# The stretch between the experts and the attention: pair swap by a DVE shuffle instead of copies, and a new order of key pieces, sums, tables and heads

## The chip, the cores and the metric

The kernel runs on one core of a Trainium2 chip, in one launch. The metric is the device time of one execution in microseconds (us). One execution was taken with the profiler; all durations and positions below are of that execution, counted from the start of its span.

The engines are named as the profile names them: PE (TensorE, matrix products; PEld is its weight load), DVE (VectorE), ACT (ScalarE), POOL (GpSimd) and SP (the queue from which most transfers are issued). Each engine works through its own list of instructions in the order in which the program wrote them, and waits on semaphores where an operand or a buffer is not ready.

## The reference

Two decoder layers with a layer norm behind each of six blocks, on `x` of 4 x 512 x 256 and a context of 4 x 1601 x 256, all in float32:

```python
x = _layernorm(x + _L0_attn_ref(...))    # per-token gradient steps
x = _layernorm(x + _L0_xattn_ref(...))   # one-head attention over the context
x = _layernorm(x + _L0_ffn_ref(...))     # 8 experts, 2 per token, each with its own norm
x = _layernorm(x + _L1_attn_ref(...))    # causal self attention, 16 heads of 16
x = _layernorm(x + _L1_xattn_ref(...))   # 16 heads, rotated queries and keys
x = _layernorm(x + _L1_ffn_ref(...))     # dequantized weights
```

The case is about the border between the third block and the next two. An expert's output is normalized and scaled with its own gamma and beta, and each token sums the rows of its two experts. In the fifth block, queries and keys of every head are rotated, where neighbouring rows are swapped in pairs (the sign is folded into the table of sines):

```python
def apply_rope(x, cos, sin):
    x2 = jnp.stack([-x[..., 1::2], x[..., 0::2]], axis=-1).reshape(x.shape)
    return x * cos + x2 * sin
```

## The kernel before, in words

Everything is written for a manual schedule: the order in which the Python code emits an instruction is its order on its engine. Line numbers are those of the kernel before.

**Experts.** Rows are sorted by expert and worked off in 23 blocks of 256 rows (`E + NDYN`). The loop runs `first_half` (both input products, gelu and sigmoid) of one block, `turned` of the next and `second_half` of the one before. `second_half` evicts the output product (L899), normalizes (L903), applies gamma and beta on POOL (L909, L910) and stores the block to `ys` from SP's queue (L911). After each `second_half` one step of the generator `attention_first` is run (`next(more, None)`): it prepares what attention needs. A step reaches to the next `yield`; there are 22 calls in the loop, and what is left of the generator runs behind the last block. Among its last steps are `live` (L989), `xa_bo` (L996) and `bob` (L1000), each a small product on PE and an eviction on DVE. Earlier steps load the context of batch 0 into the buffers `qt` and `ks`, load the rotation tables of batch 0 into `turn` buffers (the idle `xT` tiles), and fill `ng`, `vs` and `v` with memsets on POOL.

**Behind the experts.** The code at L1593 onwards writes out by hand:

- `fetch`: eight gathers on POOL of the rows of `ys` for batch 0 (tiles `ex`); `first_sums`: gathers and sums for batch 1, on POOL alone.
- the loads of the tables `c_cos` and `c_sin` (1601 columns each) on SP's queue.
- the values of batch 0 (13 tiles; L1196 copies each out on ACT).
- `keys0`, eight key pieces of batch 0: chunks 0 to 3 of the context with two pieces `c` each. `keys0[0:2]` and `[4:6]` read chunks 0 and 2, which lie in the buffers of heads' groups 0 and 1; `[2:4]` and `[6:8]` read chunks 1 and 3, in those of groups 2 and 3.
- `values1`, 13 value tiles of batch 1, from chunks `cx` (two buffers) that SP loads two ahead.
- `add`: the two weighted expert rows summed into `x` of batch 0 on DVE (L1091), with statistics (L156), root (`sd`, `rstd` on ACT, L125 and L127) and scaling on ACT; `turn`: its transposes.
- `k0_`, `q0_`, `k1_`, `q1_`: projections of self-attention keys and queries, halves 0 and 1 of the heads; each is stored to DRAM from a `raw` tile, and `rows0`, `rows1` read it back in the layout by heads, on SP's queue. `self_values(0)`: four value tiles.

**A key piece** (`key` in `context`) is a product on PE, an eviction with bias on ACT into a `raw` tile (four buffers), the rotation (`rotated`), and later a store of `raw` to `kcd` in DRAM from SP. `flush(1)` at the head of each piece issues the stores of all but the newest finished piece; `flush(0)` issues all. `rotated` fills `swp` (two buffers) with the rows of `raw` swapped in pairs, and then does two products with the tables and a sum. These three run on DVE for batch 0 and on POOL for all others and for the queries (24 key pieces and 8 queries).

**Attention.** 32 units (`units`): four head groups of four batches, first self attention, then cross attention. For each unit `slot1` computes scores only for their maxima, on PE and DVE (L1274 self, L1272 cross; tiles `one`, four banks), a few slots ahead of the unit's own scores, exponentials (L1329, ACT) and weighted sums (L1342). Other work is put into lists by unit, `extras[i]`, and run between the slots; among it are the key pieces of batches 1 to 3 (`keys1`, `later`) and the cross queries. The maxima, exponentials and these pieces share the engines in the order written.

Of the kernel before, what the change touches and what calls it, by code (L numbers as in the profile page):

```python
# [17 lines left out]
P = 128  # L18
# [21 lines left out]
def decoder(ctx: ExitStack, tc: tile.TileContext, a: dict, out: bass.AP):  # L40
# [748 lines left out]
    def const(pool, name, shape, queue):  # L789
        t = pool.tile(shape, F32, tag=name, name=name)  # L790
        queue.dma_start(t, a[name])
        return t
# [28 lines left out]
    with tc.tile_pool(name="p3", bufs=2) as p3, ExitStack() as ordered:  # L821
# [70 lines left out]
        def second_half(i, wo, xb, g):  # L892
            ps = bank()
            pv = ps.rearrange("p (h d) -> p h d", d=D)
            for h in range(2):
                blk = slice(h * P, (h + 1) * P)
                mm(pv[:, h, :], [(g[:, f, blk], wo[:, f * D : (f + 1) * D]) for f in range(NF)])
            r = p3.tile([P, 2, D], F32, tag="rb", name="rb")
            nc.vector.tensor_tensor(r, pv, xb, ALU.add)  # L899
            mv = moments(r, 2)  # L900
            rs = rstd_of(mv, eps12, 2)
            for h in range(2):
                nc.vector.tensor_scalar(  # L903
                    r[:, h, :], r[:, h, :], mv[:, h, 0:1], rs[:, h : h + 1], ALU.subtract, ALU.mult
                )
            gam, bet = (
                wo[:, None, (NF + k) * D : (NF + k + 1) * D].to_broadcast([P, 2, D]) for k in (1, 2)
            )
            nc.gpsimd.tensor_tensor(r, r, gam, ALU.mult)  # L909
            nc.gpsimd.tensor_tensor(r, r, bet, ALU.add)  # L910
            nc.sync.dma_start(ys[i * BLK : (i + 1) * BLK, :].rearrange("(h p) d -> p h d", p=P), r)  # L911

        def attention_first():
# [5 lines left out]
            ready["later"] = p4a.tile([P, 2 * P], BF16, tag="later", name="later")  # L919
            yield  # L920
            nc.gpsimd.tensor_copy(ready["later"], later)
            yield
            qt, ks = ready["qt"], ready["ks"] = [group_tiles(p4a, n, S) for n in ("qt", "ks")]

            at = qt + ks
# [24 lines left out]
            for i in range(2 * NT):  # L950
                t = p4a.tile([P, 4, 32], F32, tag=f"ng{i}", name=f"ng{i}")
                nc.gpsimd.memset(t, 0.0)
                ngs.append(t)
            yield
            ready["vself"] = [values_tile(p4a, f"vs{i}", NT) for i in range(2)]
            yield
            ready["vals"] = [values_tile(p4a, "v0", NKT)]
            yield

# [68 lines left out]
    with ExitStack() as s4:  # L1028
# [118 lines left out]
        def rotated(raw, n, ks, eng, tables=None):  # L1147

            cos, sin = tables or (cosT[:, ks], sinT[:, ks])
            swp = p4.tile([P, S + 1], F32, tag="swp", name="swp")[:, :S]  # L1150
            pairs = raw.rearrange("(a two) n -> a two n", two=2)
            into = swp.rearrange("(a two) n -> a two n", two=2)
            for i in range(2):
                nc.sync.dma_start(into[:, i, :n], pairs[:, 1 - i, :n])
            eng.tensor_tensor(raw[:, :n], raw[:, :n], cos[:, :n], ALU.mult)  # L1155
            eng.tensor_tensor(swp[:, :n], swp[:, :n], sin[:, :n], ALU.mult)
            eng.tensor_tensor(raw[:, :n], raw[:, :n], swp[:, :n], ALU.add)
# [442 lines left out]
            f()  # L1600
        for f in first_sums:
            f()
        cosT = const(p4c, "c_cos", [P, S2], nc.sync)
        sinT = const(p4c, "c_sin", [P, S2], nc.sync)
        for f in context(0, (), range(4), here=qt + kself):
            f()

        keys0 = context(0, range(4), (), here=qt + kself)
        (k0_, q0_), rows0 = self_rows(0, 0)
        (k1_, q1_), rows1 = self_rows(0, 1)  # L1610
        for f in keys0[0:2] + keys0[4:6] + values1[:6] + add + values1[6:] + turn:
            f()
        for f in (k0_, q0_, rows0, *keys0[2:4], *keys0[6:8], *self_values(0), k1_, q1_, rows1):
            f()
        flush(0)
        for i, (n0, n1) in enumerate(((0, 4), (4, 6), (6, 7), (7, 8))):
            extras[i] = keys1[n0:n1] + extras[i]
        later = [
            context(2, range(4), ()) + context(3, range(2), ()),
            context(3, range(2, 4), ()) + context(2, (), range(4)),  # L1620
# [238 lines left out]
```

## Time and profile before

| what | us |
|---|---|
| median of three runs | 2454.46 (2454.04 to 2455.28) |
| profiled execution: its own time | 2460.01 |
| profiled execution: its span | 2458.2 |
| PE busy | 2349.0 |
| DVE busy | 1187.0 |
| ACT busy | 1074.2 |
| POOL busy | 425.0 |
| mean granted TensorE clock | 0.964 of full speed |
| experts' last product on PE begins | 1013.1 |
| first self-attention maximum on DVE | 1101.6 |

The span runs from the first to the last instruction. A busy PE includes matmuls that wait in its pipeline, and at a lower granted clock the same matmul is busy for longer; so idle PE time and the clock are read together. A row of the timeline gives start, duration, engine, line, operation, output and inputs, and in brackets how long the engine had been idle before it and what ended that. Rows with SPq are issues of transfers: a long one or a late one means that the queue was waiting. Idle time of an engine that no other waits for costs nothing.

### The profile page before, as it was taken

What the parts mean: (1) busy time and instruction counts of PE and PEld (TensorE: products, weight loads), DVE (VectorE), ACT (ScalarE), POOL (GpSimd) and SP (SyncE); (2) the same over time, 40 slices, a digit from 0 to 9 for tenths busy, and PEclk for the clock granted to TensorE, in tenths of its full rate; (3) what the DMA queues carried; (4) which work ended last, traced back from release to release, by engine and by line L of the source; (5) the groups of instructions that cost most, each with busy time, mean ns of one, the idle gap of its engine ahead of it and who ended that gap; (6) DMA issues with size and microseconds to landing.
All of it is one profiled execution on the core that took longest, in us unless ns stands there. A gap on an engine that the chain in (4) does not pass through costs nothing.

```text
span 2458.2 us, 34942 instructions
## 1 busy us (share of the span) xinstructions
PE 2349.0 (96%) x13928; PEld 1331.3 (54%) x13928; DVE 1187.0 (48%) x2772; ACT 1074.2 (44%) x1996; POOL 425.0 (17%) x431
## 2 busy tenths in 40 slices
PE   7998999959999999969999999999999999999998
PEld 4767677748888888743333334333333333333256
DVE  1333334422222222336666667666666666677334
ACT  1111222114455544324555553655566565556730
POOL 1010001121134444323330000222110010000000
PEclk9999999969999999978999998999999999999999
DMA  8300211234767555442211220122210110110100
GB/s 319 135 1 23 102 54 44 73 135 149 263 251 273 212 190 197 145 122 81 83 44 30 71 75 5 49 73 62 66 54 20 44 40 16 32 36 16 33 9 26
DMA packets 82513, 224.50 MB, mean 91 GB/s; under 512 B 14120, under 2 KB 37934, under 8 KB 73262
## 3 DMA queue, kind: packets, MB, share of 16 engines
q1 hardware_dynamic: 68190, 141.70, 17.1%
q0 software_dynamic: 10992, 65.54, 7.3%
q10 hardware_dynamic: 3168, 15.03, 1.8%
q8 instruction: 110, 1.80, 0.3%
q14 instruction: 53, 0.43, 0.1%
HBM read 171.53 MB, written 53.21 MB: 91 GB/s over the span
## 4 chain that ended last, share of the span: by engine, by line
PE 51%; ACT 1%; DVE 1%; issue 0%; DVEq 0%; ACTq 0%
PE s L1315 23%; PE one L202 12%; PE po L1342 11%; PE s L202 2%; PE s L1325 1%; PE one L1300 1%; PE one L1363 1%; ACT x L171 0%; ACT ex L1329 0%; DVE one L1274 0%; PE one L1384 0%; PE one L1405 0%; PE one L1482 0%; DVE pm L1272 0%; DVE st L156 0%
## 5 line engine op out<-in xcount | busy, mean ns | idle before, releaser
L1329 ACT ACTIVATE ex<-s 128x512 f32<-128x512 f32 (+1 forms) x1062 | 578.1, 594 | 480.5 <-PE s L1315 237.4
L1272 DVE TENSOR_REDUCE pm<-one 128x1 f32<-128x512 f32 x768 | 494.2, 686 | 203.7 <-PE s L1315 147.7
L1315 PE MATMUL s<-q,kc 32*128 32x512 f32 x1612 | 522.9, 640 | 0.2 <-ACT ex L1329 0.2
L202 PE MATMUL one<-kc,qt 32*128 32x512 f32 (+1 forms) x2048 | 483.6, 563 | 0.3 <-DVE pm L1272 0.3
L1315 PEld LDWEIGHTS s<-q,kc 32*128 32x128 f32 x1612 | 161.6, 179 | 210.2 <-issue 175.2
L1342 PE MATMUL po<-ex,v 128*32 128x256 f32 (+3 forms) x2472 | 245.8, 466 | 0.3 <-ACT ot L1355 0.3
L1274 DVE CUSTOM_DVE_ANT_0 one<-one,c_diagq 128x512 f32<-128x512 f32 x256 | 172.0, 716 | 89.2 <-PE one L202 78.3
L1315 PE MATMUL s<-q,ks 32*128 32x512 f32 x512 | 182.2, 660 | 4.9 <-ACT ex L1329 4.9
L1342 PEld LDWEIGHTS po<-ex,v 128*32 128x32 f32 (+1 forms) x2472 | 49.9, 108 | 233.0 <-issue 227.0
L886 DVE TENSOR_TENSOR g<-g,sg 128x1024 f32<-128x1024 f32 x46 | 57.3, 1246 | 238.3 <-ACT sg L883 238.3
L202 PE MATMUL wide<-xbT,eWi 128*128 128x256 f32 x736 | 168.4, 388 | 4.0 <-DVE xbT L858 4.0
L202 PEld LDWEIGHTS one<-kc,qt 32*128 32x128 f32 x2048 | 163.9, 188 | 11.7 <-DVE pm L1272 7.7
L202 PE MATMUL bank<-eWo,g 128*128 128x256 f32 x736 | 162.8, 379 | 0.5 <-DVE rb L899 0.5
L202 PE MATMUL wide<-xbT,eWg 128*128 128x256 f32 x736 | 162.9, 379 | 0.1
L202 PEld LDWEIGHTS wide<-xbT,eWi 128*128 128x128 f32 x736 | 143.6, 195 | 25.1 <-issue 3.4
L1155 POOL TENSOR_TENSOR raw<-raw,c_cos 128x512 f32<-128x512 f32 (+1 forms) x32 | 35.0, 1093 | 696.2 <-DMA swp<-raw 616.5
L202 PE MATMUL one<-ks,qt 32*128 32x512 f32 x512 | 153.4, 668 | 1.1 <-ACT raw L1126 1.1
L202 PEld LDWEIGHTS wide<-xbT,eWg 128*128 128x128 f32 x736 | 139.8, 190 | 19.5 <-ACT g L883 0.5
L202 PEld LDWEIGHTS bank<-eWo,g 128*128 128x128 f32 x736 | 138.1, 190 | 18.5 <-DVE rb L899 0.6
L883 ACT ACTIVATE g<-wide,eWi 128x256 f32<-128x256 f32 x184 | 71.9, 477 | 69.8 <-PE wide L202 67.0
L1315 PEld LDWEIGHTS s<-q,ks 32*128 32x128 f32 x512 | 54.1, 188 | 83.1 <-issue 61.9
L202 PE MATMUL wide<-ctxT,q 128*128 128x512 f32 (+1 forms) x256 | 91.3, 510 | 0.8 <-DVE q L649 0.8
(310 smaller groups left out, 2969.7 us busy)
## 6 DMA issues: line engine op xcount, KB each, us to landing
xs<-zero SPq DMA_DIRECT2D x32, 512.0 KB
kc<-kcd SPq DMA_DIRECT2D x16, 800.5 KB
eWo<-in_eWo SPq DMA_DIRECT2D x8, 1408.0 KB
cx<-in_ctxT SPq DMA_DIRECT2D x18, 512.0 KB
eWi<-in_eWi SPq DMA_DIRECT2D x8, 1028.0 KB
eWg<-in_eWg SPq DMA_DIRECT2D x8, 1028.0 KB
swp<-raw SPq DMA_DIRECT2D x64, 128.0 KB
qt<-qd SPq DMA_DIRECT2D x32, 256.0 KB
```

The lines of the kernel that those rows point to most:

```text
L202: nc.tensor.matmul(ps, l, r, start=(i == 0), stop=(i == n - 1))
L883: nc.scalar.activation(dst[:, k, :], pv[:, k, :], func, bias=bias)
L886: nc.vector.tensor_tensor(part, part, dst, ALU.mult)
L1155: eng.tensor_tensor(raw[:, :n], raw[:, :n], cos[:, :n], ALU.mult)
L1272: nc.vector.tensor_reduce(pm[:, t, j, c : c + 1], ps, AX.X, ALU.max)
L1274: nc.vector.tensor_tensor_reduce(out=ps, in0=ps, in1=diagq[:, 384 - t * P : 896 - t * P], scale=1.0, scalar=LOWEST, op0=ALU.add, op1=ALU.m ...
L1300: nc.tensor.transpose(pt[:, t * P : (t + 1) * P], ng.rearrange("p j r -> p (j r)"), ident)
L1315: nc.tensor.matmul(ps[:kn], kt[rows, k * P : k * P + kn], q2[rows, :], start=True, stop=cross)
L1325: nc.tensor.matmul(ps[:, k * P : (k + 1) * P], later_[:, :P], later_[:, P:], start=False, stop=True)
L1329: nc.scalar.activation(ex[:kn, h, :], ps[:kn], AF.Exp)
L1342: nc.tensor.matmul(state["po"][j * 32 : j * 32 + 32, q0:q1], (vals if cross else vself)[b % 2][:kn, k, c0 : c0 + 32], ex[:kn, j % 2, q0:q1 ...
L1363: nc.tensor.transpose(pt[:, t * P : (t + 1) * P], ot[:, t * P : (t + 1) * P], ident)
```

## The change

Five edits, all at this border but for the last, which also reaches into attention:

- three `yield`s of `attention_first` are taken out, so that its last steps come three blocks earlier, and the memsets of `ng`, `vs` and `v` run in one step;
- the last block's gamma and beta are applied on DVE;
- the sums of batch 0 (`add`) follow two key pieces and all of `values1`; the other two pieces of groups 0 and 1 come behind the sums; self values come ahead of the remaining four key pieces, and `k1_`, `q1_`, `rows1` move into the first unit's `extras`;
- the tables `c_cos` and `c_sin` are loaded behind the last key piece of batch 0;
- `rotated` swaps the pairs with one `stream_shuffle` on DVE from `raw` to `swp` instead of two transfers on SP's queue, in all 40 rotations.

```diff
-            nc.gpsimd.tensor_tensor(r, r, gam, ALU.mult)
-            nc.gpsimd.tensor_tensor(r, r, bet, ALU.add)
+            eng = nc.vector if i == E + NDYN - 1 else nc.gpsimd
+            eng.tensor_tensor(r, r, gam, ALU.mult)
+            eng.tensor_tensor(r, r, bet, ALU.add)
...
             nc.gpsimd.tensor_copy(ready["later"], later)
-            yield
             qt, ks = ready["qt"], ready["ks"] = [group_tiles(p4a, n, S) for n in ("qt", "ks")]
...
                 ngs.append(t)
-            yield
             ready["vself"] = [values_tile(p4a, f"vs{i}", NT) for i in range(2)]
-            yield
             ready["vals"] = [values_tile(p4a, "v0", NKT)]
             yield
...
             swp = p4.tile([P, S + 1], F32, tag="swp", name="swp")[:, :S]
-            pairs = raw.rearrange("(a two) n -> a two n", two=2)
-            into = swp.rearrange("(a two) n -> a two n", two=2)
-            for i in range(2):
-                nc.sync.dma_start(into[:, i, :n], pairs[:, 1 - i, :n])
+            nc.vector.stream_shuffle(swp[:, :n], raw[:, :n], [i ^ 1 for i in range(32)])
             eng.tensor_tensor(raw[:, :n], raw[:, :n], cos[:, :n], ALU.mult)
...
-        cosT = const(p4c, "c_cos", [P, S2], nc.sync)
-        sinT = const(p4c, "c_sin", [P, S2], nc.sync)
         for f in context(0, (), range(4), here=qt + kself):
             f()
...
-        for f in keys0[0:2] + keys0[4:6] + values1[:6] + add + values1[6:] + turn:
+        for f in keys0[0:2] + values1 + add + keys0[4:6] + turn:
             f()
-        for f in (k0_, q0_, rows0, *keys0[2:4], *keys0[6:8], *self_values(0), k1_, q1_, rows1):
+        for f in (k0_, q0_, rows0, *self_values(0), *keys0[2:4], *keys0[6:8]):
             f()
+        cosT = const(p4c, "c_cos", [P, S2], nc.sync)
+        sinT = const(p4c, "c_sin", [P, S2], nc.sync)
         flush(0)
         for i, (n0, n1) in enumerate(((0, 4), (4, 6), (6, 7), (7, 8))):
-            extras[i] = keys1[n0:n1] + extras[i]
+            extras[i] = ([k1_, q1_, rows1] if i == 0 else []) + keys1[n0:n1] + extras[i]
```

## The prediction

> **What bounds the kernel now.** The page first (busy rows and slices), then the table of windows, then the timeline of the one place where the slices show a hole. In the page:
>
> ```profile
> PE 2349.0 (96%) x13928; PEld 1331.3 (54%) x13928; DVE 1187.0 (48%) x2772; ACT 1074.2 (44%) x1996; POOL 425.0 (17%) x431
> ...
> PE   7998999959999999969999999999999999999998
> ...
> PEclk9999999969999999978999998999999999999999
> ```
>
> TensorE is the bound nearly everywhere. The edit's place is the hole at slices 17 and 18, between experts and attention. The windows there (columns: window, length, busy PE, PEld, DVE, ACT, POOL, clock, DMA share, GB/s):
>
> ```profile
> 1020.00:1030.00 10.00, 6.88 (x19) 4.28 (x18) 3.30 (x10) 2.33 (x4) 3.95 (x5) 0.69 0.08 26
> ...
> 1050.00:1060.00 10.00, 3.62 (x17) 2.91 (x16) 6.75 (x10) 0.98 (x3) 6.11 (x7) 0.90 0.65 192
> 1060.00:1070.00 10.00, 3.84 (x9) 2.56 (x9) 6.29 (x16) 3.32 (x10) 8.45 (x10) 0.50 0.09 27
> ...
> 1080.00:1090.00 10.00, 6.24 (x24) 3.47 (x22) 0.00 (x0) 1.93 (x3) 0.00 (x0) 0.93 0.62 193
> ```
>
> From 1010 to 1130 TensorE is idle for 23.0 us (the sum of 10 minus PE busy over the twelve windows), and its clock is down to 0.50. What ends the idle times, from the timeline (start, duration, instruction, [idle before <- releaser]):
>
> ```profile
> 1025.48 5.03 PE L202 MATMUL one<-xaV,qt 128*128 128x256 f32 x11 [0.61 <-DVE bob L1000]
> ...
> 1059.66 3.75 PE L202 MATMUL one<-xaV,cx 128*128 128x256 f32 x8 [6.38 <-DMA cx<-in_ctxT]
> ...
> 1066.39 0.30 ACT L125 ACTIVATE sd<-mv,eps 128x4 f32<-128x4 f32 x1 [14.44 <-DVE mv L161]
> ...
> 1069.57 5.49 PE L202 MATMUL one<-xaV,cx 128*128 128x256 f32 x12 [6.16 <-ACT v L1196]
> ...
> 1087.06 1.91 SPq L1154 DMA_DIRECT2D swp<-raw  x2
> ...
> 1091.33 0.32 ACT L1187 ACTIVATE raw<-one,bk 128x65 f32<-128x65 f32 x1 [5.58 <-DMA kcd<-raw]
> 1091.70 4.02 PE L202 MATMUL one<-qkvV,xT 128*128 128x256 f32 x8 [4.76 <-ACT raw L1187]
> ...
> 1101.64 0.69 DVE L1274 CUSTOM_DVE_ANT_0 one<-one,c_diagq 128x512 f32<-128x512 f32 x1
> ```
>
> Four stalls: (1) the experts' leftovers (`live`, `xa_bo`, `bob`) hold the first value matmul until 1025.5; (2) 6.4 us for a context chunk, whose load stood on SP's queue behind `swp` copies that waited; (3) 6.2 us for ScalarE, stopped 14.4 us at `sd` because the expert sums stand in the middle of `values1`; (4) 4.8 us because `raw`'s four buffers come free only after `kcd<-raw`, which stood behind `rows0` and `swp` copies. 1101.64, the first self-attention maximum, is my finish mark.
>
> **The change, part by part.** I walk the new order with the old durations.
>
> *Three fewer yields.* `live`, `xa_bo` and `bob` ran behind the last expert and now fall into its loop. Their matmuls cost about 1.4 us there at full clock (two of 0.39 to 1.14 us and one of 1.02 at the gap's low clock), so the last expert's product, 7.17 us from 1013.1, ends near 1020.7 instead of 1020.2; its eviction (0.69 us) frees the bank and values start near 1021.4 instead of 1025.5. Thirteen value tiles took 13.9 us at a clock partly of 0.69; at 0.86 each, as `cx` tiles took at 1046, they take 11.2: done 1032.6 (was 1039.3). The merged POOL step puts 1.23 us of `ng` memsets and about 1.1 of `vs` and `v` ahead of one weight fetch instead of three; POOL sat over 9 us waiting for each `eWo`, and TensorE had no such wait. Cost 0; if that cover were gone, 1 us once. The `ctxT` loads on ScalarE's queue go one expert earlier: 0.
>
> *Last gamma and beta on DVE.* 2 x 0.69 (the `raw<-raw,xT` row) for 2 x 1.27 on POOL. With the later product `ys` is issued near 1025.5, not 1026.1: gathers 0.6 us earlier.
>
> *Sums behind two key pieces; shuffle.* Two key pieces (4 matmuls of 0.43 each, 1.75): 1036.1. DVE rotates each with a shuffle and three 0.69 operations: done 1040.7. `values1`'s first chunk to 1039.6; the third chunk's load is issued at once, since no copy stands before it on SP, and lands 3 to 4 us later: stall about 1 us instead of 6.4; `values1` done 1048.4. The sums (6.5 us on DVE, 1059.5 to 1066.0) run beside it from 1040.7 to 1047.2; the last gather is in by 1040. Root and four scalings (1066.4 to 1069.3 on ACT, 2.9 us, behind the last `v`) end at 1051.7, as TensorE ends the other two key pieces (1051.9): stall (3) gone. Two `raw` writes, transposes and copies take 2.5 us; `k0_` ends near 1056.2 and `q0_` 1058.0 (were 1078.2, 1079.9).
>
> *What is late next.* `rows0` reads back what `k0_` wrote: 4.06 us from store to read (1078.87 to 1082.93), for `q0_` too, and SP waits in order. `kcd<-raw` of the second pieces goes out near 1064.6 and lands 4.5 us later (1086.36 to 1091.33 before), so the third pieces' `raw` is written near 1069 to 71; TensorE has self values and key pieces until about 1066, then idles up to 5 us. Four rotations (2 x 2.75 + 2 x 0.9) bring DVE to 1077: the finish mark moves from 1101.6 to 1077, **-24.6**.
>
> *Heads moved into the first unit.* `k1_`, `q1_` are 8 matmuls of 0.43, 3.5 us. The unit's first loop is paced by DVE: 24 maxima at 0.65 spacing; before, it had 2.6 us of waits for TensorE inside 1101.6 to 1119.3. With two shuffles (1.4) it takes 18.7 us against TensorE's 16.8, one head being done before the mark. Loss +1.1. The loads that move with them (`rows1`, four reads of 256 KB) are needed two units later.
>
> *Tables later.* The 1.6 MB of `c_cos`, `c_sin` go behind five `cx` and two `kcd` loads, the heads' transfers and four more `kcd` stores on SP, near 1076.5, and take 5 to 8 us (at 200 to 337 GB/s, windows 1050 and 1030). Everything stored behind them lands near 1085; the next `raw` and its shuffle, which stands behind sixteen maxima (1088), are just covered. If not, DVE is held and all maxima behind it: up to 4 us. I take 0.
>
> *32 shuffles in attention.* 64 copies of 128 KB and their issues (median 0.58 us of SP) go; POOL waited 616 us for them, but POOL is not on the chain of waits, so 0 gained. DVE gains 26 of 128x512 and 6 of 128x65. No shuffle is in the trace. Lower end: the 0.43 of a 128x256 operation (`st<-x`); nearest row: `raw<-raw,xT`, 0.69 for 128x512 and 0.23 for 128x65. The Trainium skill ("VectorE: DVE Perf Modes", The perf-mode tier table) gives a shuffle only the 1x mode, about 2400 ns at 2048 elements; less 1536 cycles of its 0.96 GHz that is an estimate of 0.80 for 512. Row: 19 us of DVE; page: 23. I take the row.
>
> Here a rule speaks against the change. The same skill ("TensorE: Matmul & The Clock Gate", Architectural detail) calls DVE's queue strict FIFO: a shuffle waiting for ScalarE's `raw`, or for POOL to release `swp`, holds every maximum behind it. Before, SP and POOL did that waiting. In the trace a cross query's matmul ends at 1587.6, `raw` at 1588.5; a shuffle would end at 1589.3 and push the next pair of maxima from 1588.8 to 1589.3, ready 1590.6; the matmul that reuses the bank starts at 1591.0. So 0.4 us is left: 0 by the row, and if the cover were gone, 0.5 to 0.8 each. The FIFO with no slack would make 32 x 0.7 = +22 us. I take +1 to +3 in all, +2.
>
> Sum: -24.6 + 1.1 + 2 = **-21.5**. The profiled execution took 2460.0 (span 2458.2), 5.6 above the median of the shown runs; a difference carries over: 2454.5 - 21.5 = 2433.
>
> **The rivals.** *A, as above*: 2433, own range 2425 to 2440. For it: each stall has its releaser named, and each is moved.
> *B, half of it is given back*: another wait takes the place, most likely `raw`'s ring (stores behind the tables), or values wait for all of the experts' DVE work (4 us), the chunk or the clock: after 6 us idle it stood at 0.50, and longer waits near 1066 to 1077 could repeat that. 6 to 16 us lost: 2439 to 2449. For it: SP's order still holds four reads behind a store; against: no copies between them.
> *C, slower*: the shuffle at the head of DVE's queue holds the maxima in the attention units, and TensorE waits for banks. With 23.5 gained in the gap, it decides from 23.5 / 32 = 0.73 us lost per shuffle (slower by 0.2% from 0.89); at 1.0 us it gives 2454.5 - 23.5 + 32 = 2463. For it: FIFO, two `swp` buffers, POOL's 3.8 us per rotation; against: 0.4 us slack and DVE 65% busy there.
> *D, the gap does not move*: if only the gathers (POOL, 1029 to 1039) and their sums set it, the gap gains 0.6, and 2 is paid: 2456. Against: sums ended 3.6 us before `v` could go on, only because of where they stood.
>
> **How the numbers follow.** A 0.68, B 0.20, C 0.06, D 0.06. Within 0.2% (4.9 us, about what a measurement of this kernel can tell from no change) fall D and B's and C's edges. Faster 0.87, same 0.07, slower 0.06. Range 2424 (A with cheaper rereads) to 2448 (B's end): it leaves out C, D and a little of B and of A's lower side.
>
> **What would show it.** Right: no `bob` after the last expert; the first maximum near 1077; PE idle in 1010 to 1110 under 12 us; no `swp<-raw` on SP; shuffles of 0.7 us; windows from 1600 on still 40.00 of 40. Wrong: first maximum after 1090 (B), and its releaser; PE waits `<-DVE pm` or `<-DVE one` growing in the units (C); shuffles of 1 us or more; POOL waiting for `c_cos` past 1090.

## The result and the profile after

The changed kernel takes 2437.68 us (median of 4 runs, 2436.17 to 2439.88) against 2454.87 us before (4 runs, 2454.04 to 2462.13): a ratio of 0.9924, 95% interval 0.991 to 0.9939. In a second set of runs the same kernel took 2433.41 us against 2453.51, ratio 0.9921 (0.99 to 0.9942). So it is faster by 17 to 20 us, where the forecast said 21.5. The profiled execution of after has a span of 2438.0 us (own time 2439.88), that of before 2458.2 (2460.01).

The page of the changed kernel, busy time and slices:

```profile
PE 2344.4 (96%) x13928; PEld 1328.2 (54%) x13928; DVE 1211.7 (50%) x2854; ACT 1073.5 (44%) x1996; POOL 422.7 (17%) x429
...
PE   7898999959999999989999999999999999999998
...
PEclk9999999969999999989999997999999999999999
```

DVE has 24.7 us more work than before. The hole at slices 17 and 18 is nearly filled. The table of windows shows what is left of it (window, length, busy PE, PEld, DVE, ACT, POOL, clock, DMA share, GB/s):

```profile
1020.00:1030.00 10.00, 9.07 (x43) 7.69 (x42) 3.95 (x10) 3.62 (x8) 1.86 (x2) 1.00 0.15 52
...
1050.00:1060.00 10.00, 9.50 (x33) 6.16 (x32) 1.70 (x8) 6.13 (x15) 5.69 (x7) 0.85 0.44 134
1060.00:1070.00 10.00, 10.00 (x32) 5.92 (x32) 4.92 (x10) 3.54 (x8) 6.56 (x7) 1.00 0.44 128
1070.00:1080.00 10.00, 6.29 (x18) 2.68 (x17) 9.05 (x24) 1.32 (x3) 4.39 (x4) 0.68 0.69 213
1080.00:1090.00 10.00, 10.00 (x29) 3.62 (x28) 6.37 (x21) 1.19 (x2) 0.00 (x0) 0.81 0.60 186
```

From 1010 to 1130 TensorE is idle for 7.9 us (12 windows, 112.08 busy), against 23.0 before. What is left has names in the timeline of after (start, duration, instruction, [idle before <- releaser]):

```profile
1024.00 2.18 PE L202 MATMUL one<-xaV,qt 128*128 128x256 f32 x9 [0.93 <-DVE rb L899]
...
1048.69 6.24 PE L202 MATMUL one<-xaV,cx 128*128 128x256 f32 x20 [2.07 <-DMA cx<-in_ctxT]
...
1055.24 0.30 ACT L125 ACTIVATE sd<-mv,eps 128x4 f32<-128x4 f32 x1
...
1069.71 6.72 SPq L1054 DMA_DIRECT2D kcd<-raw  x4
...
1075.64 0.32 ACT L1182 ACTIVATE raw<-one,bk 128x65 f32<-128x65 f32 x1 [4.54 <-DMA kcd<-raw]
...
1076.01 3.47 PE L202 MATMUL one<-ks,qt 32*128 32x512 f32 x4 [2.73 <-ACT raw L1182]
...
1078.20 0.69 DVE L1269 CUSTOM_DVE_ANT_0 one<-one,c_diagq 128x512 f32<-128x512 f32 x1
```

Each of the four stalls of before has its row. (1) Nothing of `live`, `xa_bo`, `bob` stands ahead of the values: they wait for the last expert's eviction alone. (2) The wait for the chunk is 2.07 us, not 6.38. (3) The root `sd` has no wait in brackets. (4) The short key pieces still wait for a `raw` buffer, whose store to `kcd` has to land: ACT 4.54 us, and TensorE behind it 2.73. So this stall is shorter, not gone. The first maximum stands at 1078.20 instead of 1101.64.

The same stretch and the first unit behind it, once more as two windows each, first before, then after. The first window runs from the first value product to the first maximum, the second from there to the end of unit 0 (its `ot` eviction on ACT):

```profile
1025.50:1101.60 76.10, 56.73 (x183) 37.37 (x184) 20.10 (x41) 21.06 (x50) 31.18 (x35) 0.81 0.47 146
1101.60:1148.00 46.40, 46.40 (x208) 16.90 (x211) 33.35 (x106) 14.87 (x29) 15.05 (x12) 0.82 0.34 98
```

```profile
1024.00:1078.20 54.20, 47.60 (x175) 32.46 (x176) 28.61 (x67) 21.42 (x50) 32.46 (x34) 0.93 0.46 139
1078.20:1129.60 51.40, 51.02 (x216) 17.61 (x218) 36.44 (x114) 15.99 (x30) 15.06 (x12) 0.81 0.37 107
```

The stretch is 22 us shorter; the first unit is 5 us longer. In the first unit TensorE is hardly idle in either kernel, so its length splits cleanly into time lost at a reduced clock, (1 - clock) x length, and the rest: before 46.4 = 8.4 lost + 38.0, after 51.4 = 9.8 lost + 0.4 idle + 41.2. These two figures return below.

From the end of unit 0 to the end of unit 31 it is 1186.4 us before and 1184.3 after.

### The profile page after: what moved, and what is told of

The parts are those of the page before. It is cut to its first block, busy times and chain, and to the rows that moved or that the text cites. A ratio compares the mean times of both kernels' runs of the same rounds, so it can differ in the third digit from the quotient of the medians.

```text
span 2438.0 us, 34867 instructions
## 1 busy us (share of the span) xinstructions
PE 2344.4 (96%) x13928; PEld 1328.2 (54%) x13928; DVE 1211.7 (50%) x2854; ACT 1073.5 (44%) x1996; POOL 422.7 (17%) x429
## 4 chain that ended last, share of the span: by engine, by line
PE 51%; ACT 1%; DVE 1%; issue 0%; DVEq 0%; ACTq 0%
PE s L1310 23%; PE one L202 12%; PE po L1337 11%; PE s L202 2%; PE s L1320 1%; PE one L1295 1%; PE one L1358 1%; ACT x L171 0%; ACT ex L1324 0%; DVE one L1269 0%; PE one L1379 0%; PE one L1477 0%; PE one L1400 0%; DVE pm L1267 0%; DVE st L156 0%
## 5 line engine op out<-in xcount | busy, mean ns | idle before, releaser
L1269 DVE CUSTOM_DVE_ANT_0 one<-one,c_diagq 128x512 f32<-128x512 f32 x256 | 171.9, 716 | 75.6 <-PE one L202 63.5
L1337 PEld LDWEIGHTS po<-ex,v 128*32 128x32 f32 (+1 forms) x2472 | 49.8, 108 | 232.2 <-issue 225.5
L883 ACT ACTIVATE g<-wide,eWi 128x256 f32<-128x256 f32 x184 | 71.7, 476 | 72.3 <-PE wide L202 69.7
```

Source lines behind the costliest of these rows:

```text
L883: nc.scalar.activation(dst[:, k, :], pv[:, k, :], func, bias=bias)
L1269: nc.vector.tensor_tensor_reduce(out=ps, in0=ps, in1=diagq[:, 384 - t * P : 896 - t * P], scale=1.0, scalar=LOWEST, op0=ALU.add, op1=ALU.m ...
L1337: nc.tensor.matmul(state["po"][j * 32 : j * 32 + 32, q0:q1], (vals if cross else vself)[b % 2][:kn, k, c0 : c0 + 32], ex[:kn, j % 2, q0:q1 ...
```

## The experiments

Three marks are used: S, the stretch from the first value product to the first self-attention maximum; U, from there to the end of unit 0; A, from there to the end of unit 31. They come from one profiled execution each. Beside them stands a split of all runs of a kernel: time lost to the clock is the mean of span x (1 - mean granted clock) over its runs, the rest is the mean of span x clock. (Idle time at half clock is counted as half lost, so the split isn't exact where TensorE idles; in its stretch S the profile of before has about 10 us of such idle time, the 6.16 us of stall (3) and parts of its neighbours, so about 5 us of its lost time is idle time; outside S the profiles of before and after have as much of it as each other.) The standard errors of the two means are 0.8 to 3.1 and 0.2 to 1.2 us.

| kernel | median | ratio to before, 95% | S | U | A | lost | rest |
|---|---|---|---|---|---|---|---|
| before (43 runs on three chips for the split) | 2454.87 | 1 | 76.2 | 46.4 | 1186.4 | 78.7 | 2373.9 |
| changed | 2437.68 | 0.9924 (0.991 to 0.9939) | 54.2 | 51.4 | 1184.3 | 68.8 | 2367.2 |
| changed, again | 2433.41 | 0.9921 (0.99 to 0.9942) | 50.7 | 51.5 | 1185.9 | 69.7 | 2362.7 |
| e1, copies everywhere | 2435.9 | 0.9911 (0.9894 to 0.9929) | 61.7 | 48.2 | 1183.7 | 68.6 | 2366.8 |
| e2, shuffle alone | 2453.88 | 0.9994 (0.998 to 1.0008) | 69.9 | 46.2 | 1185.0 | 77.4 | 2373.6 |
| e3, copies in attention | 2428.08 | 0.9882 (0.9866 to 0.9897) | 51.4 | 46.7 | 1180.3 | 63.7 | 2361.7 |
| e4, attention's shuffles twice | 2440.14 | 0.9927 (0.9914 to 0.9939) | 50.8 | 51.2 | 1191.8 | 67.8 | 2369.8 |
| e5, old order of key pieces and sums | 2439.83 | 0.9929 (0.9913 to 0.9945) | 59.1 | 50.7 | 1187.4 | 69.9 | 2369.5 |
| e6, other heads before the unit | 2434.04 | 0.9928 (0.9906 to 0.9949) | 50.4 | 49.7 | 1184.3 | 70.6 | 2362.4 |
| e7, short pieces' `raw` elsewhere | 2433.86 | 0.991 (0.9884 to 0.9937) | 48.8 | 48.4 | 1186.5 | 64.0 | 2365.6 |
| e8, three yields back | 2441.08 | 0.9942 (0.992 to 0.9963) | 51.2 | 47.6 | 1180.3 | 71.0 | 2366.6 |
| e12, attention's rotations deferred | 2439.57 | 0.9939 (0.9918 to 0.996) | 50.9 | 50.5 | 1192.4 | 74.3 | 2363.2 |
| e13, e3 and e7 together | 2428.59 | 0.9889 (0.9868 to 0.991) | 49.0 | 48.8 | 1182.9 | 63.1 | 2363.1 |
| e14, copies in unit 0 only | 2430.53 | 0.9907 (0.9886 to 0.9928) | 49.8 | 45.7 | 1182.8 | 65.2 | 2364.1 |

The changed kernel lies between 2430.91 and 2439.88 from run to run, and its rest differs by 4.5 us between its two sets, so one profile alone decides nothing that is smaller than about 3 us, unless the row of a wait names it. The profiles of e1 (2445.4) and e5 (2447.85) were the slowest of their six runs.

**The changed kernel again**, unedited, on the chip of e6, e7 and e12:

> The changed kernel once more, unedited, beside the others of this call, because the parts ahead of the edit moved by some us between executions. All theories: 2436 to 2442, and first maximum 50 to 55 us behind the first value matmul.

It repeats the ratio; the median, 2433.41, is under the 2436 to 2442 that were expected. S is 3.5 us shorter than in the first profile, since the chunk's wait of 2.07 us is 0.50 there; U is the same.

**e2: the shuffle alone.** Before, with one edit:

```diff
-            for i in range(2):
-                nc.sync.dma_start(into[:, i, :n], pairs[:, 1 - i, :n])
+            nc.vector.stream_shuffle(swp[:, :n], raw[:, :n], [i ^ 1 for i in range(32)])
```

> The kernel before with the shuffle alone: order of key pieces, sums, tables, other heads, yields and the last tile's factors all as before. Theory (shuffle and order each bring their share in the gap): the waits of TensorE for raw behind the copies (0.69, 4.76 and 1.14 us) go, the waits for the late chunk and for the sums (6.38 and 6.16 us) stay, so first value to first self maximum is 65 to 70 us, against 76.2 before and 50.7 to 54.2 changed; attention's shuffles take back 3 to 8 us, ratio 0.997 to 1.001. Rival (the copies were behind all of the waits, the sums' too, through the queues): first value to first maximum under 62 us, ratio under 0.995. Rival on the other side: VectorE, on which the key pieces still stand ahead of the sums, now carries the shuffles too, and the sums end later than 1069.6 us: ratio over 1.001.

The ratio is 1 and S is 69.9, both where the theory had them. Its account of the waits was wrong, though. TensorE's idle rows in e2, from the timeline:

```profile
1058.20 1.97 PE L202 MATMUL one<-xaV,cx 128*128 128x256 f32 x8 [2.08 <-DMA cx<-in_ctxT]
1066.43 4.97 PE L202 MATMUL one<-xaV,cx 128*128 128x256 f32 x12 [6.26 <-ACT v L1193]
...
1089.58 3.78 PE L202 MATMUL one<-qkvV,xT 128*128 128x256 f32 x8 [5.57 <-ACT raw L1184]
```

and the row of ScalarE that released the last of them:

```profile
1089.21 0.32 ACT L1184 ACTIVATE raw<-one,bk 128x65 f32<-128x65 f32 x1 [6.38 <-DMA kcd<-raw]
```

The chunk's wait fell from 6.38 to 2.08 us: the copies had held its load on SP. The wait for the sums stayed (6.16 before, 6.26 here): order alone makes it. And the wait for `raw` did not go, it grew from 4.76 to 5.57: with no copies left on SP, the `kcd` store still lands late. It stood behind `rows0` (the reads of `ks` and `qt`), not behind the copies, as SP's rows in e2 show:

```profile
1082.92 0.42 SPq L1059 DMA_DIRECT2D qt<-qd  x1
1083.44 3.54 SPq L1056 DMA_DIRECT2D kcd<-raw  x4
```

**e1: all but the shuffle.** The changed kernel with the two copies back in all 40 rotations (the diff of e2 turned round):

> The changed kernel with only the shuffle undone: all 40 pair swaps are two transfers on SP's queue again; order, tables, heads, gamma and yields stay changed. Theory (order and shuffle work together): in the gap a swap costs 3.5 us from issue to use instead of 0.73, and the copies of the third and fourth pieces stand on SP behind the reads of rows0 and the stores of the pieces before, so the first maximum comes 6 to 10 us later than 1078.2 and the kernel takes 2443 to 2448 against 2437.7. Rival 1 (the order did it all, nothing waits for the swap): first maximum within 2 us of 1078, kernel 2437 to 2439. Rival 2 (the shuffle did it all): back at 2453 or more.

S is 7.5 us longer than in the first profile of the changed kernel and 11 longer than in the second, as expected. But the kernel isn't slower, where the theory had 2443 to 2448: the median is 2435.9 and the ratio 0.9911, against 0.9924 and 0.9921 with the shuffle. So over the whole kernel the other edits together bring all of the gain, with 40 shuffles or with none. e1 and e2 say the same from both sides.

**e3: shuffle in the gap, copies in attention.**

```diff
+            if tables:
+                nc.vector.stream_shuffle(swp[:, :n], raw[:, :n], [i ^ 1 for i in range(32)])
+            else:
                 ...
+                for i in range(2):
+                    nc.sync.dma_start(into[:, i, :n], pairs[:, 1 - i, :n])
```

> The changed kernel with the shuffle kept for the eight pieces of batch 0 and the copies on SP again for the 32 rotations in the attention units. Theory (DVE has cover there): the distance from the end of unit 0 to the end of the kernel is the same within 1 us, so 2436.5 to 2438.5. My forecast's term was a cost of 2 for these shuffles: then 2435.7. Rival C (shuffles hold the maxima, 0.3 us or more each): 2428 or less. Other rival (the copies cost something on SP or in the transfers): above 2440.

This is the fastest version of all: 2428.08 us, ratio 0.9882, whose interval ends (0.9897) below where those of the changed kernel begin (0.991 and 0.99). On the same chip it is 7.8 us under e1 in the medians, and 10.1 in the means (standard error 2.7): that is what the eight shuffles of the gap are worth. And about as much, 7 us by the mean spans of this set and of the changed kernel's second one and 10 us by the ratios, is what the 32 in attention cost. The split says how. Against the changed kernel's second set, the rest fell by 1.0 us (2362.7 to 2361.7) and the time lost to the clock by 6.0 (69.7 to 63.7).

The time is about where rival C had it, but not for its reason. Here is A in one window each, for before, the changed kernel and e3:

```profile
1148.00:2334.40 1186.40, 1176.29 (x8691) 426.79 (x8692) 763.86 (x1614) 678.92 (x1287) 156.35 (x143) 0.98 0.15 45
1129.60:2313.80 1184.20, 1174.08 (x8691) 426.61 (x8691) 779.11 (x1670) 678.60 (x1286) 156.25 (x143) 0.99 0.13 40
1117.60:2297.90 1180.30, 1170.19 (x8691) 427.06 (x8692) 763.50 (x1614) 678.42 (x1287) 156.18 (x143) 0.99 0.15 45
```

TensorE is idle for 10.1 us in each, so the shuffles hold it up nowhere in A. The trace also lists every change of the clock. Counted in pieces of 3.41 us at half clock (they are worked out in the last section), A holds 12 before, 10 and 11 in the two profiles of the changed kernel, and 8 in e3. Less the 1.7 us that each of them costs, A is 1165.9 us before, 1167.2 and 1167.1 changed, and 1166.6 in e3. Outside the clock, then, attention's shuffles cost A about 1 us. The counts of single profiles don't tell copies from shuffles, though: e8, with shuffles, has 7, and e13, with copies, 10. That takes the means over all runs, which follow under e8.

**e4: each of attention's 32 shuffles twice**, the second one repeating the first:

```diff
+            if not tables:
+                nc.vector.stream_shuffle(swp[:, :n], raw[:, :n], [i ^ 1 for i in range(32)])
```

> The changed kernel with each of the 32 shuffles in the attention units done twice, the same result written a second time: 20.6 us more on DVE (26 of 0.73, 6 of 0.23), each directly behind the first, with the maxima behind it. In the trace the next maxima came 0.5 us late at most and the bank was wanted 0.4 us after that, so a second 0.73 overruns the cover by about 0.3 us in some places. Theory (cover): 0 to +4 us, 2438 to 2442, and the units without a shuffle unchanged. Rival (no cover, DVE's time goes straight to the end): +15 to +21, 2453 to 2459.

Some 20.3 us more of VectorE (26 x 0.73 + 6 x 0.23) give a ratio of 0.9927, inside the changed kernel's interval. In the split the rest is 2.6 to 7.1 us higher than in the changed kernel's two sets, and A 6 to 7.5 us longer; the time lost is not higher. So VectorE's time as such costs some 0.1 to 0.25 us per shuffle, once the slack has been used by the first 32. The cost that e3 removes isn't of this kind.

**e14: copies in unit 0 only.** Four pieces (numbers 9 to 12) use the copies, the other 36 the shuffle:

```diff
+            turned[0] += 1
+            if 9 <= turned[0] <= 12:
+                ...
+            else:
+                nc.vector.stream_shuffle(swp[:, :n], raw[:, :n], [i ^ 1 for i in range(32)])
```

> The changed kernel with only the four key pieces of unit 0 swapped by DMA copies; the other 36 pieces stay with the shuffle. Theory 'first unit' (the cost of attention's shuffles lies in the first unit, where one more spell of half clock follows): maximum to the end of unit 0 is 46 to 48.5 us, against 51.4 and 51.5 of the changed kernel's two profiles, the rest of attention stays at 1184 to 1192 us, ratio 0.990 to 0.991. Theory 'spread' (each shuffle costs a little on VectorE's queue, 28 of them after the first unit): first unit gains at most 1 us, ratio 0.992 to 0.993, and only copies in all 32 pieces bring 0.988.

U is 45.7, slightly better than the theory of the first unit had it, and the ratio of 0.9907 falls where that theory had it, though its interval also holds 0.992. The windows of U, the second profile of the changed kernel, then e14:

```profile
1073.70:1125.20 51.50, 51.12 (x216) 17.70 (x218) 36.40 (x114) 16.05 (x31) 15.07 (x12) 0.81 0.35 104
```

```profile
1074.10:1119.90 45.80, 45.80 (x216) 16.20 (x218) 33.00 (x106) 16.01 (x31) 15.05 (x12) 0.89 0.46 141
```

The same 216 matmul records, without idle time, at a clock of 0.89 instead of 0.81: 5.0 us lost instead of 9.8. What remains is 40.8 and 41.3. So nearly all that U gains is clock.

**e8: the three yields back.** It was meant for the yields, and tells something of U too.

> The changed kernel with the three yields of the tile generator put back, so that live, the factors of its biases and one memset batch run behind the last expert again. Theory: the values begin later against the last expert gelu: 24.5 to 26 us instead of 20.5, and nothing behind takes it back: gelu to the end of unit 0 127 to 131 us against 122.8 and 126.1, ratio 0.9935 to 0.995. Rival (the third context chunk sets the pace behind the values anyway, so that a later start only shortens the wait for it): first value to first maximum 2 to 4 us shorter than the changed kernel's 50.7 to 54.2, ratio 0.992.

```diff
             nc.gpsimd.tensor_copy(ready["later"], later)
+            yield
...
                 ngs.append(t)
+            yield
             ready["vself"] = [values_tile(p4a, f"vs{i}", NT) for i in range(2)]
+            yield
```

From the last expert's gelu to the first value it is 27.4 us, against 20.5 in both profiles of the changed kernel: worse by 6.9. But the gelu itself comes 2.5 us earlier in e8, since the leftovers don't stand in the loop ahead of it (the rows are in the next section), so taking the yields out is worth 4.4 us at the first value. The ratio of 0.9942 is in the expected place, but its interval overlaps that of the changed kernel. From the gelu to the end of unit 0 it is 126.2 us, under the 127 to 131 that were expected, because U is 47.6 here, with every shuffle in place:

```profile
1078.30:1125.90 47.60, 47.23 (x216) 16.58 (x218) 36.18 (x114) 16.02 (x31) 15.02 (x12) 0.90 0.37 113
```

So a short U doesn't need the copies; it needs the clock, and an execution can have it with the shuffles. What the copies change is how often. The kernels with copies in unit 0 and the new order with the shuffle in the gap (e3, e13, e14) lose 63.1 to 65.2 us to the clock in the mean of their runs. Of those with the shuffle there, the changed kernel, e4, e5, e6 and e8 lose 67.8 to 71.0 and e12 74.3. Only e7, at 64.0 with a standard error of 3.1, falls out of the pattern. With e7 counted in, too, the 16 runs with copies lose 64.0 us in the mean and the 48 with shuffles (both sets of the changed kernel, e4 to e8 and e12) 69.6: 5.6 less, with a standard error of 1.1. e1, with copies everywhere, loses 68.6, but its S has twice the idle time of the changed kernel's (10.0 us against 5.2 in the second profile).

**e5: the old order of key pieces and sums**, the rest as changed:

```diff
-        for f in keys0[0:2] + values1 + add + keys0[4:6] + turn:
+        for f in keys0[0:2] + keys0[4:6] + values1[:6] + add + values1[6:] + turn:
```

> The changed kernel with the sums of batch 0 in their old place: four key pieces first, then six value tiles, the sums, and the other seven value tiles. Theory (the place of the sums was one of the stalls): ScalarE stops at the root until the sums end, now near 1056 because four rotations stand before them on DVE instead of two, the last value tiles wait, and TensorE idles 3 to 6 us more; transposes and heads follow the root by one queue of seven value tiles (6 us): kernel +4 to +7, 2442 to 2445. Rival (with shuffles the sums end early enough anyway): within 1.5 us of 2437.7.

S is 4.9 and 8.4 us longer than in the two profiles of the changed kernel. In the medians this is hardly seen (0.9929); in the split the rest is 2.3 and 6.8 us higher. The direction holds; the size is between these.

**e6: `k1_`, `q1_`, `rows1` before the first unit again**:

> The changed kernel with k1_, q1_ and rows1 back in front of the first unit (behind the last key pieces of batch 0), all else as changed. From first maximum to first exponential the changed kernel takes 26.4 us and the kernel before 22.7. Theory (two heads at half clock among DVE's maxima cost 2 to 4 us, and their old place costs as much, because raw's buffers come free only when the stores of the third pieces have landed, near 1077 and 1081): within 2 us of after_again. Rival (moving the heads was a gain of their full 3.5 to 7 us on TensorE): +3.5 to +7. Other rival (the move was a loss): -2 to -4.

```diff
-        for f in (k0_, q0_, rows0, *self_values(0), *keys0[2:4], *keys0[6:8]):
+        for f in (k0_, q0_, rows0, *self_values(0), *keys0[2:4], *keys0[6:8], k1_, q1_, rows1):
```

S and then U, in the profile of e6:

```profile
1021.80:1072.20 50.40, 47.65 (x180) 32.28 (x180) 27.67 (x66) 21.72 (x50) 29.13 (x31) 0.99 0.48 148
1072.20:1121.90 49.70, 49.05 (x212) 18.75 (x214) 36.87 (x114) 15.97 (x30) 17.48 (x16) 0.77 0.36 112
```

S is as long as in the second profile of the changed kernel (50.7) although it holds the heads' products too: TensorE idles 2.8 us instead of 5.2, since they fill part of the hole at the short key pieces. U without idle time and time lost is 37.6, as before (38.0), against 41.3 in the changed kernel: the heads are 3.3 to 3.6 us of TensorE wherever they stand. Moving them gains nothing: 0.9928.

**e7: the short pieces' `raw` from the tiles of `q2`**, so that they don't wait for a store:

```diff
+        def raw_tile(aside=False):
+            if aside:
+                return p4.tile([P, S], F32, tag="q2", name="raw_q2")
...
-                raw = raw_tile()
+                raw = raw_tile(here is not None and i == 3)
```

> The changed kernel with the two short pieces of batch 0 (65 columns, the last ones in front of the first unit) evicted into the two q2 tiles, which are free then, instead of the third round of raw's four buffers. It takes away ScalarE's wait for the stores (4.5 us at 1075.6) and with it TensorE's 2.7 and 0.9 us ahead of the first unit, without any other edit. Theory (that wait stops TensorE, which then does the heads at half clock, and DVE waits 3.5 us for them): first maximum 1 us earlier, first exponential 3 to 5 us earlier against after_again, kernel -3 to -5. Rival (DVE, rotating until 1077, sets the start anyway): -1 or less.

S is 48.8, 1.9 us below the second profile of the changed kernel; TensorE's row `<-ACT raw` is gone, and the next wait stands in its place:

```profile
1073.65 4.02 PE L202 MATMUL one<-ks,qt 32*128 32x512 f32 x8 [2.83 <-DVE pm L1271]
```

It is the wait for the first maxima (the first at 1072.85), which stand behind the last rotations on VectorE. From the last gelu to the end of unit 0 it is 117.8 us against 122.8, yet the ratio (0.991, 0.9884 to 0.9937) can't be told from the changed kernel's.

**e13: e3 and e7 together.**

> Two edits at once: the 32 swaps of attention are DMA copies again, and the two short key pieces of batch 0 take their raw from the tiles of q2. Theory 'clock' (what both edits save is spells of half clock, about 6 us long and worth about 3 us of TensorE's work each, that follow an idle TensorE or thin work in the first unit): the edits save at different places, so they add: first value to first self maximum at most 49.5 us, maximum to the end of unit 0 at most 47, ratio to before 0.985 to 0.987. Rival (both edits remove the same spell): first unit as with the copies alone, 46 to 48 us, ratio 0.988 as with the copies alone or no better. Second rival (the copies' gain of the first run was chance of that chip): ratio 0.991 to 0.993, as of the changed kernel.

Ratio 0.9889, no better than e3's 0.9882: the two edits don't add, as the first rival had it. S gained its 2 us; U is 48.8, above all that was expected and 2 us longer than in e3, so the gain of S is used up at the end of U. The ratio repeats that of e3 on another chip, which speaks against chance.

**e12: attention's rotations put off by one piece**, so that no shuffle waits at the head of VectorE's queue for a fresh `raw`:

```diff
-                rotated(raw, kw, slice(k0, k0 + kw), eng, ready["turn", i] if here else None)
-                going.append(lambda: to_rows(kcd[b], c, k0, kw, raw[:, :kw]))
+                ...
+                    later_turned(raw, kw, slice(k0, k0 + kw), eng, store=store)
```

> The changed kernel with the shuffle of each of the 32 rotations in the attention units issued one piece later (at the head of the next key piece or query, or before the reads), with the rotation on POOL behind it; the same instructions, DVE does as much, but raw has long been written when the shuffle comes to the head of DVE's queue. Theory F (the wait at the head of DVE's queue costs, not DVE's time): the time of e3_attn_copies, 2427 to 2432, and DVE's wait for raw in the units, 37 us in the changed kernel, falls under 5. Theory W (the work or something else about the shuffle costs): within 2 us of after_again. Theory N (the gap between e3_attn_copies and the others is only clock and transfers by chance): e12 and after_again the same, too.

U is only 1 us shorter (50.5). The edit brought a cost of its own: one step of 9.2 us between units 13 and 14, where a deferred shuffle and store now stand directly ahead of the reads that need them. Its start is a row of TensorE:

```profile
1432.50 0.77 PE L202 MATMUL one<-kc,qt 32*128 32x65 f32 x10 [1.90 <-DMA qt<-qd]
```

The wait itself is 1.90 us; from 1434.4 the clock then stands at half for 13.7 us, which costs 6.8 more. The test of the wait at the head of the queue is therefore inconclusive; it gives no support to it.

## Why the prediction came out as it did

The time was forecast at 2433.0 and the range at 2424 to 2448; 2437.68 lies inside. The mechanism of the gap was right: the stalls went, or grew shorter, where it said. Two terms had the wrong size, the leftover products in the experts' loop and the heads in the first unit. That the sum came so near is in part luck, since other terms erred the other way.

*Values earlier.* 4.1 us were forecast, with the leftovers' matmuls put at about 1.4 us in the loop. The loop's last three blocks, from the last gelu of the block before them to the last gelu of all, take 63.5 us in each of the three profiles with the old yields (before, e2, e8) and 66.0 in each of the eleven without them. So the leftovers cost 2.5 us there, where TensorE is never idle, and not 1.4. The last of the three blocks, before and then after:

```profile
984.46 7.07 PE L202 MATMUL bank<-eWo,g 128*128 128x256 f32 x32
991.37 7.07 PE L202 MATMUL wide<-xbT,eWi 128*128 128x256 f32 x32
```

```profile
987.54 7.07 PE L202 MATMUL bank<-eWo,g 128*128 128x256 f32 x32
994.55 0.69 PE L202 MATMUL bank<-xa_bo,ones 1*128 1x256 f32 x2
995.17 7.17 PE L202 MATMUL wide<-xbT,eWi 128*128 128x256 f32 x32
```

From start to start of the two large products it is 6.91 and 7.63 us. From the last gelu to the first value it is 25.9 us before and 20.5 after, so 5.4 are gained there and 2.9 in all (e8 puts it at 4.4, with the other edits in place). The merged memsets cost nothing visible. That the values begin at 1024.0 and not at 1021.4 is 1.2 us from this term and 1.4 from the part of the execution ahead of these three blocks, which ends anywhere between 933.0 and 940.0 us in the fourteen profiles.

*The stretch to the first maximum, -24.6.* In positions it is -23.4 (1101.64 to 1078.20). Counted from the gelu ahead of those three blocks it is 165.55 us before and 140.70 after, so -24.85, and -28.36 in the second profile. In the first profile the sum was met, its steps less so. The chunk stalls 2.07 and 0.50 us where 1 was forecast. The sums are covered. `k0_` ends at 1061.72, its forecast end was 1056.2: 2.6 of the 5.5 us come from the values' start, 1.4 from the chunk (2.07 + 0.32 idle against 1), and 1.7 from half clock behind the chunk's wait (1049.6 to 1053.0), which the forecast put into rival B alone. From the end of `k0_` to the mark it took 16.5 us where the forecast allowed 20.8, and the wait for `raw` came later than said: not at the third pieces (1069 to 71) but at the short ones (1075.64).

*Which edit.* The prediction put stall (4) down to `rows0` and the copies together, and e2 shows that without the copies it is as long as ever. The shuffle removes 4.3 us of stall (2) by itself (6.38 to 2.08), and its other gains need the new order. (Of the 64 copies in attention, which the prediction gives as 128 KB each, the 12 for the short pieces have 16 KB; nothing in the sum hangs on it.)

*Heads in the first unit, +1.1.* This step failed in size. It took the loop as paced by VectorE's maxima, with the heads' 3.5 us of matmuls beside them. Measured, U grew by 5.0 us: 3.2 of matmuls (38.0 to 41.2; e6 gives 3.3 to 3.6 by moving them back), 0.4 of idle time and 1.4 of clock (8.4 to 9.8). TensorE's time in U is full, so what is added to it is added to the end. The prediction read the waits of VectorE for TensorE in that loop, and not TensorE's own row, which had 46.40 of 46.40 us.

*32 shuffles, +2.* One shuffle takes 0.728 us, and the mask for it is a row of its own of 0.01 us (columns: duration in ns, least, median, most; first and last start; forms):

```profile
L1149 DVE LOAD_MASK_SELECT swp<-raw x40: 7/14/14, 1038.0 to 2086.4; - x40
L1149 DVE STREAM_SHUFFLE swp<-raw x40: 225/728/748, 1038.0 to 2086.4; 128x512 f32<-128x512 f32 x32, 128x65 f32<-128x65 f32 x8
```

That is between the row taken (0.69) and the page's estimate (0.80), nearer the row. The slack held in the units: TensorE's idle time in A is 10.1 us as before. The waits of shuffles in attention, in total, times and longest, are those of VectorE alone:

```profile
DVE swp L1149 <- ACT raw L1182: 26.7, 16, 3.0
DVE swp L1149 <- ACT raw L1212: 10.3, 8, 1.5
```

Hardly any of it reaches TensorE: before the cross maxima's products it is idle for 0.3 us in all (busy, mean ns | idle before):

```profile
L202 PE MATMUL one<-kc,qt 32*128 32x512 f32 (+1 forms) x2048 | 483.8, 564 | 0.3 <-DVE pm L1267 0.3
```

So rival C had its mechanism, a shuffle that waits at the head of VectorE's queue, but no price to TensorE. A without the time lost to the clock grew by about 1.2 us, near the +2. What the sum lacked is the clock: with copies in all of attention or in unit 0 alone the kernel loses 3.6 to 6.0 us less to it (e3 and e14 against the two sets of the changed kernel). So the +2 is about right for VectorE's time, and beside copies in the same place attention's shuffles cost 7 to 10 us all the same. By the ratios e14 finds 3 to 4 us of it in unit 0 alone. Rival B named the clock, but as something that a long wait near 1066 to 1077 would bring once; it came back twice more where TensorE shows no wait at all. The kernel before had that, too: its U lost 8.4 us, with TensorE busy throughout. So the shuffles didn't bring the loss into U; the profiles with copies there in the new order (e3, e13, e14) lose less than before, 5 to 7 us.

*The tables.* `c_cos` and `c_sin` were issued at 1076.48 and 1076.98, as forecast near 1076.5. The first rotation on POOL starts at 1097.43, 0.08 us behind the end of its shuffle. The profile puts its wait down to a load of `cx`, which it doesn't read; a wait for the tables is not seen.

*The whole.* From the gelu ahead of the last three blocks to the end of unit 0 it is 211.9 us before and 192.1 after, so -19.8; in the second profile 188.7, -23.2. The forecast for this was -24.6 + 1.1 = -23.5. In the first profile the stretch gave what was forecast and the first unit gave back 3.9 us more than that. The attention behind gave -2.1 where +2 was forecast, because two fewer pieces of half clock fell into it (-3.4), which no term foresaw. With +1.4 from the part ahead and +0.3 at the end this makes the -20.2 of the two spans (2458.2 to 2438.0). So it is luck that the error of the first unit was made good in A. The profiled execution of before stood 5.1 us above its median and that of after 2.2: hence -17.2 in the medians.

What stays open: where in attention the remaining 3 to 6 us of e3's gain lie (e14 against e3; their intervals overlap), and why copies leave the clock up more often. e8's profile shows that the shuffles don't force the loss, so it is a matter of how often; the deferral of e12, which could have shown the place, cost something of its own.

## What to carry to other kernels

Before work is moved out of a gap, look at the row of the bounding engine in the place it is moved to: if that engine is busy there in full, the work is moved and not hidden (3.2 us of the heads' matmuls and 2.5 us for the leftovers here). A copy by DMA that nobody waits for can be better than an engine instruction: in the gap the shuffle brought 8 to 10 us; in attention, where the copies lay behind everything else, the same shuffle cost about as much, most of it in the clock and not in a wait that any row shows. Split each length into idle time, time lost to the clock, and the rest, over all runs, before looking for a stall that explains a few microseconds.

## What the runs showed of the hardware

*The clock falls in fixed pieces.* The end of U's last slow spell in the first profile of the changed kernel, in windows of 2 us (clock third from the right):

```profile
1102.00:1104.00 2.00, 2.00 (x8) 0.85 (x8) 2.00 (x7) 0.00 (x0) 1.92 (x3) 1.00 0.60 70
1104.00:1106.00 2.00, 2.00 (x11) 1.14 (x10) 1.97 (x8) 1.09 (x2) 1.19 (x1) 0.56 0.67 236
1106.00:1108.00 2.00, 2.00 (x8) 0.63 (x4) 1.82 (x5) 0.42 (x1) 0.00 (x0) 0.50 0.52 150
1108.00:1110.00 2.00, 2.00 (x3) 0.67 (x2) 0.98 (x5) 0.67 (x2) 0.00 (x0) 0.50 0.18 70
1110.00:1112.00 2.00, 2.00 (x10) 0.31 (x8) 0.00 (x0) 0.69 (x1) 0.00 (x0) 0.74 0.00 0
```

The clock is 1 or one half. Half clock held here for (0.44 + 0.50 + 0.50 + 0.26) / 0.5 x 2 = 6.8 us, which cost 3.4 us. The spell from 1073.5 is worked out in the same way as 10.2 us. It began 0.2 us after TensorE had run out of work at 1073.3, so before most of the idle 2.73 us at the short pieces had passed. The Trainium skill ("TensorE: Matmul & The Clock Gate", What's actually happening) gives the gate two states and a free-running window of 3413 ns; 6.8 and 10.2 us are two and three of these, so trace and page agree. The traces' lists of clock changes say it more sharply: in all fourteen profiles each change lies on one grid of 3.413 us, and half clock lasts from 1 to 12 of its steps. One window at half clock costs 1.7 us.

*It fell with TensorE busy in the records.* In U of the changed kernel TensorE was idle for 0.4 us in all, and the clock fell twice: from 1087.1 to 1090.6 TensorE is busy throughout, and from 1090.6 the clock is at half. (A matmul that waits in the pipeline counts as busy.) The matmuls of these 3.5 us use 32 of the 128 rows and go at the pace of VectorE's maxima; that this is too little activity for the gate is argued, not shown.

*Identical code differs by whole windows.* Six runs of e7 have clocks from 0.970 to 0.979 and times from 2436.12 to 2419.46 us; over the runs of one kernel, time rises by 0.6 to 1.06 us per us lost (0.3 in e4 and 0.4 in the four runs of the changed kernel's first set). A comparison of single executions is a comparison of how many such windows each happened to lose.
